# Signs, squares and their sums of a graph layer's closing algebra on ScalarE, block by block, and one wide product folded into a small one

## The chip, the cores and the metric

The kernel runs on one core of a Trainium2 chip. The metric is the device time of one execution in microseconds (us). The median of three runs of the kernel before is 815.14 us, with 815.1 and 816.52 as lowest and highest.

## What is computed

The reference is a chain of four graph layers on 4096 nodes with 64 features and a dense 4096 x 4096 matrix of zeros and ones. Each layer adds to `x` the result of a graph operator on the normalised, rectified `x`. The change touches only the last operator, a hyperbolic one:

```python
def weighted_midpoint_lincomb(A, X):
    gamma = lambda_x(X)
    num = A @ (gamma * X)
    den = A @ (gamma - 1.0)
    sgn = jnp.where(den >= 0.0, 1.0, -1.0)
    den = sgn * jnp.maximum(jnp.abs(den), DEN_EPS)
    two_mean = num / den
    mid = mobius_scalar_mul(0.5, two_mean)
    alpha = jnp.sum(A, axis=1, keepdims=True)
    return mobius_scalar_mul(alpha, mid)
...
XW = mobius_matvec(W, X)
AXW = weighted_midpoint_lincomb(A_hat, XW)
return expmap0(jax.nn.relu(logmap0(AXW)))
```

All the norms, tanh and artanh act on one length per node. What is needed for each node is the length of the sum vector, the length of its rectified part once the sign of the denominator is applied, the denominator and the row sum `alpha`; the result is a positive factor per node times the rectified vector.

## The kernel before

The 4096 nodes lie on 128 partitions in 32 blocks, each with 64 features along the free dimension. Layer 3 treats them in eight tiles of four blocks (CB = 4), numbered u = 0 to 7. For each tile, `sum3` multiplies the adjacency matrix by a 196-column matrix on TensorE: three bf16 parts of the 64 scaled features and of the denominator's column, 65 columns each, and a column of ones for `alpha`. The function `take3` then copies the first part out of PSUM on ScalarE and adds the other two on VectorE, and so makes a tile `n65` (128 x 4 x 65) and `alpha` (128 x 4).

`layer3` (lines 1678 to 1708) fixes the order on TensorE: the first half of the sums of tiles 0 to 2, then tiles 3 to 5 in full, then the second half of tiles 0 to 2, and last tiles 6 and 7. `summed` (line 1712) gathers finished tiles. Tiles 3, 4 and 5 form the first group that is closed together, tiles 0, 1 and 2 the second; tiles 6 and 7 are closed each alone. So `post3` (line 1740) runs four times, with nb = 12, 12, 4 and 4 columns of statistics.

Inside `post3`, the work of one tile is three wide operations and a reduction: `n65` times the sign of the denominator in place (line 1753), its square on ScalarE (1755), the square of its positive part on VectorE (1756), and one `tensor_reduce` over both (1759). Then follow small operations on all columns together: `lengths` takes a reciprocal root by VectorE steps, `artanh2` uses Ln on ScalarE and a polynomial on VectorE, and a tanh closes the factor `a`. While Ln and a table load run, `between` multiplies the rectified tile by its reciprocal length (1771). After the tanh, the tile is multiplied by `a` (1779), added to `x` (1781) and written out (1782).

The order of the instructions on each engine is settled when the program is built, by a planner, `Weave`. A generator such as `post3` yields its operations one by one; the planner books each with a planned cost (`Engine.cost`: on ScalarE 0.2 us and 0.9 ns per element, 0.08 more for an accumulator) and puts it between the operations of other pieces of work where its inputs should be ready. `take3` is called directly; it first lets ready pieces run and then enters its own operations. On the chip each engine works its list in that order: an operation that waits holds back all that stand behind it. Operations that go through the planner all have line 781 in the profile, so they are told apart by their tiles: `n` is `n65`, `ss` the sums of squares, `rc` the reciprocals and what artanh2 makes of them, `ny` the reciprocal lengths, `void` a dummy that loads a table ahead.

Of the kernel before, what the change touches and what calls it, by code (L numbers as in the profile page):

```python
# [12 lines left out]
AF = mybir.ActivationFunctionType  # L13
ALU = mybir.AluOpType
AX = mybir.AxisListType
# [556 lines left out]
CB = 4  # L572
# [219 lines left out]
def fast_kernel(ctx: ExitStack, tc: tile.TileContext, t: dict, out: bass.AP, flag: bass.AP):  # L792
# [36 lines left out]
    def b2(name, shape=(P, QB, D), dtype=F32):  # L829
        return b2p.tile(list(shape), dtype, tag="b2", name=name)  # L830

    def stat(name, n):
        return small.tile([P, ST], F32, tag="st", name=name)[:, :n]
# [3 lines left out]
    DV, AC, GP, SY = (Engine(weave, x.e, x.real, True) for x in (V, S_, G_, Y_))  # L837
# [79 lines left out]
    def rows(s, width=D):  # L917
        return s[:, :, None].to_broadcast([P, s.shape[1], width])
# [12 lines left out]
    def recip(v):  # L931
        r = stat("rc", v.shape[1])
        yield DV.reciprocal(r, v)
        return r
# [632 lines left out]
    def lengths(s):  # L1567

        yield DV.tensor_scalar(s, s, NORM_EPS2, None, op0=ALU.max)
        r = yield from rsqrt(s)  # L1570
        n = stat("norm", s.shape[1])
        yield DV.tensor_tensor(n, s, r, ALU.mult)
        return n, r
# [5 lines left out]
    def preload(func):  # L1579

        yield AC.activation(void, tab, func)

    def artanh2(x, between=()):

        nb = x.shape[1]
        xc = stat("axc", nb)
        yield DV.tensor_scalar(xc, x, ARTANH_BOUND, None, op0=ALU.min)
        r = stat("at", nb)
        yield DV.tensor_scalar(r, xc, -1.0, 1.0, op0=ALU.mult, op1=ALU.add)
        q = yield from recip(r)  # L1590
        yield DV.scalar_tensor_tensor(q, xc, 1.0, q, op0=ALU.add, op1=ALU.mult)
        yield AC.activation(q, q, AF.Ln)
        yield from preload(AF.Tanh)
        low = small.tile([P, ST], I32, tag="st", name="flow")[:, :nb]
        yield DV.tensor_scalar(low, xc, 0.25, None, op0=ALU.is_lt)
        x2, p = stat("x2", nb), stat("po", nb)
        yield DV.tensor_tensor(x2, xc, xc, ALU.mult)
        yield DV.tensor_scalar(p, x2, *(2.0 * c for c in ARTANH_POLY[:2]), op0=ALU.mult, op1=ALU.add)
        yield DV.tensor_tensor(p, p, x2, ALU.mult)
        for c in ARTANH_POLY[2:-1]:  # L1600
            yield DV.scalar_tensor_tensor(p, p, 2.0 * c, x2, op0=ALU.add, op1=ALU.mult)
        yield DV.scalar_tensor_tensor(p, p, 2.0 * ARTANH_POLY[-1], xc, op0=ALU.add, op1=ALU.mult)
        yield from between
        yield DV.copy_predicated(q, low, p)
        return q
# [106 lines left out]
    def summed(u, parts3, alone=False):  # L1712
        group.append((u, parts3))
        if alone or len(group) == 3:
            weave.add(post3(group[:]))
            group.clear()
# [23 lines left out]
    def post3(parts3):  # L1740

        nb = CB * len(parts3)
        sgn, den, ss = stat("sgn", nb), stat("den", nb), stat("ss", 2 * nb)
        part = [slice(i * CB, (i + 1) * CB) for i in range(len(parts3))]
        vs = [n65[:, :, :D] for u, (n65, al) in parts3]
        for h, v, (u, (n65, al)) in zip(part, vs, parts3):  # L1750
            d = n65[:, :, D]
            yield DV.tensor_scalar(sgn[:, h], d, 0.0, 2.0, op0=ALU.is_ge, op1=ALU.mult)
            yield DV.scalar_tensor_tensor(v, rows(sgn[:, h]), -1.0, v, op0=ALU.add, op1=ALU.mult)
            sq = b2("sq")
            yield AC.activation(sq[:, :CB, :], v, AF.Square)
            yield DV.scalar_tensor_tensor(sq[:, CB:, :], v, 0.0, v, op0=ALU.max, op1=ALU.mult)
            yield DV.tensor_scalar(den[:, h], d, -1.0, DEN_EPS, op0=ALU.mult, op1=ALU.max)
            yield DV.tensor_tensor(den[:, h], den[:, h], d, ALU.max)
            yield DV.tensor_reduce(ss.rearrange("p (k b) -> p k b", k=2)[:, :, h],
                                   sq.rearrange("p (k b) d -> p k b d", k=2), AX.X, ALU.add)  # L1760
        yield from preload(AF.Ln)
        rd = yield from recip(den)
        n, r = yield from lengths(ss)
        t = stat("t", nb)
        yield DV.tensor_tensor(t, n[:, :nb], rd, ALU.mult)
        ratio = stat("ratio", nb)

        def between():
            yield DV.tensor_tensor(ratio, n[:, nb:], r[:, :nb], ALU.mult)
            for h, v in zip(part, vs):  # L1770
                yield DV.scalar_tensor_tensor(v, v, 0.0, rows(r[:, nb:][:, h]), op0=ALU.max, op1=ALU.mult)

        a = yield from artanh2(t, between())
        for h, (u, (n65, al)) in zip(part, parts3):
            yield DV.scalar_tensor_tensor(a[:, h], a[:, h], 0.25, al, op0=ALU.mult, op1=ALU.mult)
        yield DV.scalar_tensor_tensor(a, a, ARTANH_MAX, ratio, op0=ALU.min, op1=ALU.mult)
        yield AC.activation(a, a, AF.Tanh)
        for h, v, (u, (n65, al)) in zip(part, vs, parts3):
            yield DV.tensor_tensor(v, v, rows(a[:, h]), ALU.mult)
            x = X[u // 2][:, (u % 2) * CB:(u % 2 + 1) * CB, :]  # L1780
            yield DV.tensor_tensor(x, x, v, ALU.add)
            yield SY.dma_start(out_nm[:, u * CB:(u + 1) * CB, :], x)
# [103 lines left out]
```

## Time and profile before

| | value |
|---|---|
| median of three runs | 815.14 us |
| span of the profiled execution | 813.9 us |
| TensorE busy | 776.2 us |
| VectorE busy | 638.4 us |
| ScalarE busy | 397.4 us |
| mean granted TensorE clock | 0.989 |

In the profile PE is TensorE, PEld its weight load, DVE VectorE, ACT ScalarE, SP the queue of the output's transfers. A row of a group or of the timeline names the engine, the operation, the tile that is written and the tiles that are read, their shapes and how many there are. A bracket shows for how long the engine was idle before it and what released it. The chain follows the last instruction back to what released each step.

### The profile page before, as it was taken

The numbers are of one execution on the slowest core, as the hardware profiler recorded it, in microseconds if no ns is written. First come the engines' busy times: TensorE is split into PE (matmuls) and PEld (weight loads), VectorE is DVE, ScalarE is ACT, GpSimd is POOL, SyncE is SP. The second block draws the span as 40 slices with busy tenths as digits, with TensorE's granted clock in tenths as the row PEclk, the third lists the DMA queues.
The fourth block names the chain that finished last, engine by engine and source line by source line (L and its number), as shares of the span: only waits on it lengthen the run. The fifth ranks groups of instructions, "written<-read, shape, count | busy, mean of one in ns | idle before, by whom it ended". The sixth has DMA issues, their size and how long they took to land.

```text
span 813.9 us, 12101 instructions
## 1 busy us (share of the span) xinstructions
PE 776.2 (95%) x4473; PEld 358.6 (44%) x4494; DVE 638.4 (78%) x1433; ACT 397.4 (49%) x613; POOL 61.1 (8%) x125
## 2 busy tenths in 40 slices
PE   5999999999999999999999999999999999999990
PEld 1334444444433333333333334444444444699990
DVE  6886777677678798888888888878779787774896
ACT  5655555565565657666666663022120254452333
POOL 3333232230000000000000000000000000000000
PEclk9999999999999999999999999999999999999995
DMA  9999999998301032022022016797879900000010
GB/s 220 151 176 168 201 160 192 196 161 186 104 14 39 0 118 65 0 91 65 0 66 91 0 33 239 287 319 229 283 263 356 273 23 4 2 2 1 2 41 17
DMA packets 43954, 98.39 MB, mean 121 GB/s; under 512 B 5104, under 2 KB 20464, under 8 KB 43888
## 3 DMA queue, kind: packets, MB, share of 16 engines
q1 hardware_dynamic: 25888, 78.98, 29.0%
q0 software_dynamic: 15840, 14.42, 18.9%
q10 hardware_dynamic: 2160, 4.14, 1.4%
q8 instruction: 37, 0.61, 0.3%
q14 instruction: 29, 0.24, 0.1%
HBM read 135.54 MB, written 5.24 MB: 173 GB/s over the span
## 4 chain that ended last, share of the span: by engine, by line
PE 90%; DVE 6%; ACT 1%; issue 1%; DMA 1%; SPq 0%; DVEq 0%; ACTq 0%
PE acc L976 54%; PE cnt L976 14%; PE score L976 14%; PE rz L976 2%; DVE sig L781 2%; PE ih L976 1%; PE ps_t L980 1%; PE ps_l L976 1%; DMA whole<-in_adjT 1%; PE ps_kq L976 1%; DVE ss L781 1%; DVE nt L781 1%; ACT sig L781 1%; PE ps_n L980 1%; DVE rc L781 0%
## 5 line engine op out<-in xcount | busy, mean ns | idle before, releaser
L781 ACT ACTIVATE sig<-score,fatt_add,fatt_mul 128x1024 f32<-128x1024 f32 x128 | 147.9, 1200 | 85.4 <-PE score L976 84.8
L781 DVE TENSOR_TENSOR sig<-sig,A 128x1024 f32<-128x1024 f32 x128 | 151.3, 1221 | 38.7 <-ACT sig L781 37.9
L781 DVE SCALAR_TENSOR_TENSOR whole<-whole 128x1024 f32<-128x1024 f32 x128 | 153.2, 1218 | 6.0 <-DMA whole<-in_adjT 5.6
L781 ACT ACTIVATE w<-cnt 128x512 int16<-128x512 f32 x198 | 111.2, 595 | 89.9 <-PE cnt L976 88.7
L976 PE MATMUL score<-qd,kT 64*128 64x512 f32 x512 | 128.2, 617 | 0.0
L976 PE MATMUL acc<-sig,S 128*64 128x512 f32 x512 | 125.4, 606 | 1.5 <-DVE sig L781 1.4
L976 PE MATMUL acc<-A,hm 128*128 128x512 fp8e4 x512 | 115.6, 379 | 0.8 <-DVE X L781 0.8
L976 PEld LDWEIGHTS <-hm 128*128 128x128 bf16 x768 | 73.5, 98 | 90.7 <-issue 10.5
L976 PE MATMUL cnt<-A,ftri 128*128 128x512 fp8e4 x256 | 97.9, 385 | 8.3 <-ACT A L781 8.3
L976 PE MATMUL cnt<-A,fupd 128*128 128x512 fp8e4 x248 | 95.6, 386 | 2.7 <-DVE w L781 1.6
L976 PE MATMUL acc<-S,A 128*128 128x196 bf16 x1024 | 88.2, 246 | 0.0
L976 PEld LDWEIGHTS <-A 128*128 128x128 fp8e4 x1024 | 87.1, 96 | 1.1 <-issue 0.8
L976 PEld LDWEIGHTS score<-qd,kT 64*128 64x128 f32 x512 | 43.7, 186 | 80.9 <-ACT sig L781 39.1
L781 DVE TENSOR_SCALAR w<-cnt 128x512 int16<-128x512 f32 x58 | 40.1, 691 | 45.5 <-PE cnt L976 41.1
L976 PE MATMUL acc<-w,hm 128*128 128x512 bf16 x235 | 71.0, 379 | 0.9 <-issue 0.2
L860 POOL DMA_DIRECT2D A<-in_adjT x110 | 59.3, 541 | 119.7 <-DMA A<-in_adjT 118.8
L976 PEld LDWEIGHTS acc<-sig,S 128*64 128x64 f32 x512 | 30.4, 136 | 82.7 <-issue 39.5
L976 PEld LDWEIGHTS <-lo 128*64 128x64 bf16 x768 | 36.9, 109 | 58.4 <-issue 36.4
L976 PE MATMUL acc<-A,lo 128*64 128x512 fp8e4 x512 | 59.3, 380 | 0.0
L781 ACT ACTIVATE mt<-acc 64x512 f32<-64x512 f32 x32 | 18.9, 591 | 66.2 <-PE acc L976 39.6
L976 PEld LDWEIGHTS <-fupd 128*128 128x128 bf16 x248 | 24.4, 98 | 46.0 <-issue 24.3
L1647 POOL MEMSET S<- 128x4 bf16 x8 | 0.9, 116 | 550.6 <-PE ps_l L976 505.4
(185 smaller groups left out, 649.5 us busy)
## 6 DMA issues: line engine op xcount, KB each, us to landing
whole<-in_adjT SPq DMA_DIRECT2D x128, 512.0 KB, 7.0
A<-in_adjT POOLq DMA_DIRECT2D x110, 128.0 KB, 13.2
qd<-qs SPq DMA_DIRECT2D x16, 128.0 KB, 3.0
mx<-gs SPq DMA_DIRECT2D x16, 128.0 KB, 8.1
xT<-gs SPq DMA_DIRECT2D x8, 256.0 KB, 7.6
x<-in_x SPq DMA_DIRECT2D x6, 256.0 KB, 6.1
xs<-x SPq DMA_DIRECT2D x4, 256.0 KB, 4.8
qs<-qT ACTq DMA_DIRECT2D x4, 256.0 KB, 6.3
```

The lines of the kernel that those rows point to most:

```text
L781: return fn(*args, **kw)
L860: nc.gpsimd.dma_start(A8[q][b // 2][:, b % 2, :], a)
L976: nc.tensor.matmul(o, lhsT, rhs, start=start, stop=stop, skip_group_check=True)
L980: nc.tensor.transpose(o, src, ident)
L1647: nc.gpsimd.memset(S3[q, c][:, :, 3 * e:], 1.0)
```

## The change

For the groups of three tiles (nb > CB) the wide operations of a tile on VectorE are replaced by three ScalarE activations for each of its four blocks of 64 features. The first squares the block and adds the squares up in the accumulator. The second applies the sign and rectifies in place, by the activation's per-partition scale. The third squares that and adds up. The sign itself becomes two small VectorE operations. The two tiles closed alone keep the old form of this part.

For all tiles, the wide product with the reciprocal length under Ln goes. That length is multiplied into the small factor `a` after the tanh instead, and the final wide product rectifies on the way. The aim is to take work from VectorE while TensorE is still at work on later tiles.

```diff
-        for h, v, (u, (n65, al)) in zip(part, vs, parts3):
+        for i, (h, v, (u, (n65, al))) in enumerate(zip(part, vs, parts3)):
             d = n65[:, :, D]
             yield DV.tensor_scalar(sgn[:, h], d, 0.0, 2.0, op0=ALU.is_ge, op1=ALU.mult)
-            yield DV.scalar_tensor_tensor(v, rows(sgn[:, h]), -1.0, v, op0=ALU.add, op1=ALU.mult)
             sq = b2("sq")
-            yield AC.activation(sq[:, :CB, :], v, AF.Square)
-            yield DV.scalar_tensor_tensor(sq[:, CB:, :], v, 0.0, v, op0=ALU.max, op1=ALU.mult)
+            if nb > CB:
+
+                yield DV.tensor_scalar(sgn[:, h], sgn[:, h], -1.0, None, op0=ALU.add)
+                for j in range(CB):
+                    k = i * CB + j
+                    yield AC.activation(sq[:, j, :], v[:, j, :], AF.Square, accum_out=ss[:, k:k + 1])
+                    yield AC.activation(v[:, j, :], v[:, j, :], AF.Relu, scale=sgn[:, k:k + 1])
+                    yield AC.activation(sq[:, j, :], v[:, j, :], AF.Square, accum_out=ss[:, nb + k:nb + k + 1])
+            else:
+                yield DV.scalar_tensor_tensor(v, rows(sgn[:, h]), -1.0, v, op0=ALU.add, op1=ALU.mult)
+                yield AC.activation(sq[:, :CB, :], v, AF.Square)
+                yield DV.scalar_tensor_tensor(sq[:, CB:, :], v, 0.0, v, op0=ALU.max, op1=ALU.mult)
             yield DV.tensor_scalar(den[:, h], d, -1.0, DEN_EPS, op0=ALU.mult, op1=ALU.max)
             yield DV.tensor_tensor(den[:, h], den[:, h], d, ALU.max)
-            yield DV.tensor_reduce(ss.rearrange("p (k b) -> p k b", k=2)[:, :, h],
-                                   sq.rearrange("p (k b) d -> p k b d", k=2), AX.X, ALU.add)
+            if nb == CB:
+                yield DV.tensor_reduce(ss, sq, AX.X, ALU.add)
...
             yield DV.tensor_tensor(ratio, n[:, nb:], r[:, :nb], ALU.mult)
-            for h, v in zip(part, vs):
-                yield DV.scalar_tensor_tensor(v, v, 0.0, rows(r[:, nb:][:, h]), op0=ALU.max, op1=ALU.mult)
...
         yield AC.activation(a, a, AF.Tanh)
+        yield DV.tensor_tensor(a, a, r[:, nb:], ALU.mult)
         for h, v, (u, (n65, al)) in zip(part, vs, parts3):
-            yield DV.tensor_tensor(v, v, rows(a[:, h]), ALU.mult)
+            yield DV.scalar_tensor_tensor(v, v, 0.0, rows(a[:, h]), op0=ALU.max, op1=ALU.mult)
             x = X[u // 2][:, (u % 2) * CB:(u % 2 + 1) * CB, :]
             yield DV.tensor_tensor(x, x, v, ALU.add)
```

## The prediction

> **What bounds the kernel now.** I read the page's busy times and chain first, then the stretches of the last 100 us, then the chain in order of time, and last the timeline of VectorE and ScalarE there. From the page:
>
> ```profile
> PE 776.2 (95%) x4473; PEld 358.6 (44%) x4494; DVE 638.4 (78%) x1433; ACT 397.4 (49%) x613; POOL 61.1 (8%) x125
> ...
> PE 90%; DVE 6%; ACT 1%; issue 1%; DMA 1%; SPq 0%; DVEq 0%; ACTq 0%
> ```
>
> TensorE sets the time for 90% of the span. The edit is in the closing algebra of layer 3, so only that stretch counts. The busy time by stretches, columns PE, PEld, DVE, ACT, POOL:
>
> ```profile
> 740.00:760.00 20.00, 20.00 (x237) 19.80 (x236) 8.35 (x27) 3.39 (x14) 0.00 (x0) 1.00 0.01 2
> ...
> 780.00:790.00 10.00, 10.00 (x121) 10.00 (x119) 9.10 (x46) 4.92 (x14) 0.00 (x0) 1.00 0.01 2
> 790.00:800.00 10.00, 3.18 (x38) 2.95 (x35) 8.56 (x42) 3.83 (x8) 0.00 (x0) 0.77 0.13 43
> 800.00:814.00 14.00, 0.00 (x0) 0.00 (x0) 7.28 (x37) 3.59 (x7) 0.00 (x0) 0.50 0.07 22
> ```
>
> TensorE has no gap and full clock up to 793.2, so nothing that the edit frees can bring that point forward. What follows is a tail of 20.7 us. The chain in order of time:
>
> ```profile
> 758.74 34.46 PE acc L976 x404
> 793.22 0.28 ACT n L781
> ...
> 794.21 0.27 DVEq L1706
> 794.48 0.09 issue
> 794.56 0.18 DVE rc L781
> ...
> 800.90 0.42 DVE X L781
> ...
> 807.50 0.44 DVE n L781
> 807.96 0.42 DVE X L781
> ```
>
> The tail is the two tiles closed alone, one after the other: tile 6 from its reciprocal at 794.56 to its residual sum at 800.90, tile 7 to 807.96, then the output. Tile 6's sums were complete long before (ScalarE copied its last part out of PSUM at 782.7, and VectorE had added it up by 786); it is late because VectorE was busy with the second group of three (tiles 0 to 2). The timeline shows where that group stood:
>
> ```profile
> 773.67 0.21 ACT L781 ACTIVATE rc<-rc 128x12 f32<-128x12 f32 x1 [1.76 <-DVE rc L781]
> ...
> 781.85 0.16 DVE L781 TENSOR_SCALAR ss<-ss 128x24 f32<-128x24 f32 x1
> ...
> 788.97 0.21 ACT L781 ACTIVATE rc<-rc 128x12 f32<-128x12 f32 x1 [1.76 <-DVE rc L781]
> ```
>
> The tanh of the first group (tiles 3 to 5) ends at 773.9; the second group's sums of squares are ready at 781.85; its tanh ends at 789.2, 4 us before TensorE ends. That slack is what the edit can spend.
>
> **What the Trainium skill says.** "ScalarE: Activation LUTs", section "What ACT_TABLE_LOAD costs", prices an ACTIVATE at 186 ns + 0.833 ns per element, 93 ns more for each per-partition pointer operand, and lets neighbours overlap by about 93 ns. This trace agrees: 128x256 squares take 415 ns and 128x512 ones 624 ns; the tanh with a bias pointer takes 719 ns where the plain square takes 624; a square at 719.46 lasting 0.62 is followed at 719.98, an overlap of 0.10. Its 1283 ns table load is the trace's 1.28 us. "VectorE: DVE Perf Modes", section "The TRN2 errata", says that many small tiles pay a fixed latency each; the slope from 415 to 624 ns leaves some 206 ns fixed, so a 64-wide ACTIVATE is mostly overhead. "Trace Analysis", section "Optimizing Scalar/DVE Operations", says moving work to ScalarE may pay if VectorE is saturated. VectorE is near that here (9.10 of 10), but the path also runs through ScalarE.
>
> **The change part by part.** Per tile of a group, VectorE loses the wide sign product (0.42), the relu-square (0.42), the reduction (0.68) and the wide product by the reciprocal length (0.36 in steady flow), and gains small operations of 0.16 to 0.2. That is some 1.5 us per tile, or 4.5 us per group. Pricing what ScalarE gains:
>
> - A 64-wide square by the trace's slope: 415 - 192 x 0.816 = 258 ns, 0.26. The relu has a pointer scale: 0.26 + 0.095 = 0.355.
> - The relu overwrites the block that the first square reads, and the second square reads what the relu wrote; both wait for ScalarE's own completion, so overlap is lost (gap about 0.03). Only the next block's first square can follow at once (overlap 0.10).
> - The read-out of an accumulator on ScalarE is not in this trace. VectorE's is: 0.08 us (at 757.34). Lower bound 0 (free), upper 0.20, the length of ScalarE's shortest ACTIVATE (void, 203 ns). I take 0.10, a shortest ACTIVATE less its overlap.
> - One block: 0.26 + 0.10 + 0.03 + 0.355 + 0.03 + 0.26 + 0.10 - 0.10 = 1.035 us. Bounds 0.835 and 1.235. Before, a whole tile of four blocks cost ScalarE 0.42.
>
> Now the walk, by the order in which the changed program lists each engine's instructions.
>
> *First group.* Its signs start at 757.74 as before; the relus can begin at 758.1. Twelve blocks are 12.4 us, the first square runs ahead (-0.3), and the evictions of tiles 0 and 1 stand between the blocks (2 x 0.55, from 760.65 to 761.2 in the old timeline). ScalarE ends at 771.3. PSUM is released by these evictions, at latest about 771 for tile 1, whose banks tile 7 needs only at some 782 (11 us of products before the end), so TensorE is not held.
>
> *Closing of the first group.* Old second group: 781.85 to the end of the logarithm's input at 785.44 is 3.59, less 0.52 for tile 6's sums inside it, 3.07. The sums of tile 2 (two of 0.35, one of 0.43, a small one) now stand there: 1.25. Then logarithm 0.3, table load and void 1.5, which covers the polynomial (some 1.45), then five small operations and the tanh: 6.5 in all. Tanh ends at 777.8.
>
> *Second group.* Its first square is queued behind that tanh on ScalarE. 12.4 us of blocks, 0.5 for tile 6's evictions, 0.3 of waiting for the third tile's sign (VectorE forms it only after tile 6's sums): 791.0. Its sums of squares are thus ready 9.2 us later than the 781.85 of before. From there 5.85 to the end of the tanh (3.07, then tile 6's relu-square 0.35 and the rest as above): 796.9.
>
> *Behind it on VectorE.* In order: a small one and tile 7's first-half sums (0.6), the new 128x12 product (0.2), tile 0's product and residual (0.8), tile 7's last sums (0.65 with a small one), the flag read (0.35, as 794.21 to 794.56), tile 1's product and residual (0.8), tile 6's reduction (0.6), tile 2's product and residual (0.8), and only then tile 6's reciprocal: 801.6 against 794.56, +7.0.
>
> *The two lone tiles.* They keep the old form but lose 0.35 of wide product under the logarithm and gain 0.2 after the tanh. In tile 6 the copy starts about 0.25 earlier; in tile 7 the void's end at 806.97 holds the tanh anyway. Net about -0.1 each, -0.2.
>
> Sum: 7.0 - 0.2 = +6.8 us, 815.14 + 6.8 = 822.0. With the bounds of the block: at 0.835 ScalarE ends the groups at 768.9 and 786.5, and the reciprocal starts at 797.1, +2.4 net; at 1.235, 773.7, 795.8 and 806.4, +11.6 net.
>
> **The rivals.** *A floor only.* Suppose ScalarE is as quick as needed. Tile 7's last sums still cannot start before 793.6, and behind them now stand 2.2 us (two products with residuals and the reduction) that VectorE had done before: 793.59 + 0.6 + 0.35 + 2.2 = 796.75, +2.2, less 0.2: 817.1. For it: ScalarE is busy only 4.92 of 10 us in the old stretch. Against: two rounds of twelve blocks with self-waits. *A dearer read-out.* If it costs 0.28 net twice, a block takes 1.4 us, 24 x 0.36 = 8.8 more: 831; nothing here shows it, nothing excludes it. *Faster.* The 4.5 us saved per group let tile 6 close before TensorE ends; only tile 7's chain is left, and the tail loses the 6.4 us from 794.56 to 800.90: 808.7. For it: VectorE is the busy engine, and tile 6's data is there at 786. Against: the listing puts tile 6's reciprocal behind tile 7's last sums. *No change:* the queue shift is absorbed and only -0.2 stays, 814.9; no slack in the tail speaks for it.
>
> **How the numbers follow.** ScalarE becomes the pace, 822.0: 0.64. The floor, 817.1 to 817.5: 0.19. Dearer read-out, 828 and more: 0.09. Faster, 808.7: 0.04. No change: 0.04. Predicted is the first. The range from 816.8 (the floor less some rounding) to 827.0 (a block at the upper bound) leaves out the last three, 0.17. A time within 0.2% lies between 813.5 and 816.8; the floor is barely over it, so I give 0.05 to same, 0.04 to faster, 0.91 to slower.
>
> **What would show it.** TensorE still ends at about 793. ScalarE is near full from 758 to 771 and from 778 to 791, with about 1.03 us per block; a read-out row of its own tells its price. VectorE waits for ScalarE at the maximum of the 24 sums, twice. Tile 6's reciprocal starts near 801.6, and the two lone chains take 6.8 and 7 us as before. I am wrong if a block takes under 0.85 us (then 817), if TensorE is held for a PSUM bank (then later still), or if tile 6's chain is under way before 794.

## The result

The changed kernel takes 821.9 us (821.06 to 822.9) against 815.26 us for the kernel before. The ratio is 1.0079, with a 95% interval from 1.0061 to 1.0097: slower by 0.8%, some 6.4 us. The prediction was 822.0 us. The executions of each kernel fall into two clusters more than 1 us apart (815.1 to 815.4 and 816.5 before; 821.1 and 822.7 to 822.9 changed), and the profiled ones took 815.69 and 821.12 us.

The spans of the two profiles differ by 5.3 us (819.2 and 813.9). In the profiles of the kernels below, the copy of tile 5 out of PSUM, which lies ahead of the changed code, starts up to 2.0 us earlier or later than in the kernel before; so wherever times of different kernels stand in one table below, they are shifted to have that copy at 754.91, where it is in the kernel before (at 754.82 in the changed one).

### The profile page after: what moved, and what is told of

The parts are those of the page before. It is cut to its first block, busy times and chain, and to the rows that moved or that the text cites. A ratio compares the mean times of both kernels' runs of the same rounds, so it can differ in the third digit from the quotient of the medians.

```text
span 819.2 us, 12202 instructions
## 1 busy us (share of the span) xinstructions
PE 776.2 (95%) x4473; PEld 358.6 (44%) x4494; DVE 630.1 (77%) x1417; ACT 416.5 (51%) x727; POOL 61.5 (8%) x125
## 4 chain that ended last, share of the span: by engine, by line
PE 84%; DVE 9%; ACT 4%; issue 2%; DMA 1%; SPq 0%; DVEq 0%; ACTq 0%
PE acc L976 49%; PE score L976 14%; PE cnt L976 14%; PE rz L976 2%; ACT sq L781 2%; DVE sig L781 2%; PE ih L976 1%; PE ps_t L980 1%; PE ps_l L976 1%; ACT n L781 1%; DMA whole<-in_adjT 1%; DVE nt L781 1%; DVE ss L781 1%; DVE n L781 1%; PE ps_kq L976 1%
```

## The profile after

The page of the changed kernel, busy times and shares of the chain by engine:

```profile
PE 776.2 (95%) x4473; PEld 358.6 (44%) x4494; DVE 630.1 (77%) x1417; ACT 416.5 (51%) x727; POOL 61.5 (8%) x125
...
PE 84%; DVE 9%; ACT 4%; issue 2%; DMA 1%; SPq 0%; DVEq 0%; ACTq 0%
```

TensorE does the same work in the same busy time. VectorE lost 8.3 us of work and ScalarE gained 19.1, and yet the chain's share of TensorE fell from 90% to 84%: the chain now leaves TensorE at 754.8, some 38 us before TensorE's end, and runs on over ScalarE and VectorE. The stretches show where, with the columns PE, PEld, DVE, ACT and POOL, for the changed kernel:

```profile
758.00:771.00 13.00, 13.00 (x156) 12.80 (x154) 5.34 (x28) 12.20 (x67) 0.00 (x0) 1.00 0.00 1
771.00:778.00 7.00, 7.00 (x85) 7.00 (x84) 6.02 (x35) 3.96 (x13) 0.00 (x0) 1.00 0.01 2
778.00:793.00 15.00, 15.00 (x178) 14.85 (x175) 7.53 (x37) 12.59 (x64) 0.00 (x0) 1.00 0.08 28
793.00:801.00 8.00, 0.09 (x1) 0.00 (x0) 7.08 (x34) 3.85 (x10) 0.00 (x0) 0.66 0.11 37
801.00:820.00 19.00, 0.00 (x0) 0.00 (x0) 11.13 (x62) 5.58 (x11) 0.00 (x0) 0.50 0.07 23
```

Two of these rows for the kernel before:

```profile
758.00:771.00 13.00, 13.00 (x155) 12.80 (x153) 12.04 (x56) 5.40 (x16) 0.00 (x0) 1.00 0.01 1
...
778.00:793.00 15.00, 15.00 (x179) 14.95 (x176) 13.86 (x63) 5.33 (x15) 0.00 (x0) 1.00 0.08 28
```

In both groups the load changed sides: VectorE from 12.0 to 5.3 and from 13.9 to 7.5 us, ScalarE from 5.4 to 12.2 and from 5.3 to 12.6. TensorE is not held anywhere before its end. One block on ScalarE, in the timeline of the changed kernel:

```profile
759.11 0.35 ACT L781 ACTIVATE n<-n,sgn 128x64 f32<-128x64 f32 x1
...
759.49 0.26 ACT L781 ACTIVATE sq<-n 128x64 f32<-128x64 f32 x1
759.65 0.19 ACT L781 ACTIVATION_READ_ACCUMULATOR sq<-n 128x1 f32 x1
759.74 0.24 ACT L781 ACTIVATE sq<-n 128x64 f32<-128x64 f32 x1
759.89 0.18 ACT L781 ACTIVATION_READ_ACCUMULATOR sq<-n 128x1 f32 x1
760.11 0.35 ACT L781 ACTIVATE n<-n,sgn 128x64 f32<-128x64 f32 x1
```

From one rectification to the next it is 1.00 us. Each accumulator output is an instruction of its own, called the read-out here. It begins 0.15 to 0.16 after its square and the next square 0.09 after it. Where the next instruction waits (759.74 to 760.11), square and read-out cost 0.37.

The four points that the prediction walked through, in the timeline of the changed kernel:

```profile
776.96 0.21 ACT L781 ACTIVATE rc<-rc 128x12 f32<-128x12 f32 x1 [0.35 <-DVE rc L781]
...
789.92 0.18 DVE L781 TENSOR_SCALAR ss<-ss 128x24 f32<-128x24 f32 x1 [2.79 <-ACT sq L781]
...
795.52 0.21 ACT L781 ACTIVATE rc<-rc 128x12 f32<-128x12 f32 x1 [0.39 <-DVE rc L781]
...
800.22 0.17 DVE L781 RECIPROCAL rc<-den 128x4 f32<-128x4 f32 x1
```

The bracket of the second line is the new wait: VectorE stands idle for 2.79 us until ScalarE has the second group's last sum. All that stands behind it waits too: the square of tile 6's positive part, whose input was ready at 786.6, runs at 793.06. At the first group's maximum of the sums (770.47) there is no such bracket, because VectorE had waited before: for the copies of tiles 0 and 1, which stand between the blocks on ScalarE (2.71, 1.22, 1.74 and 0.84 us). The reciprocal in the last line, which opens tile 6's closing, stood at 794.56 before. The end of the chain, in order of time:

```profile
798.03 0.44 DVE n L781
798.49 0.42 DVE X L781
798.91 0.60 DVE ss L781
799.51 0.34 DVE n L781
799.88 0.42 DVE X L781
...
813.12 0.43 DVE n L781
813.58 0.42 DVE X L781
```

The first five lines are work between tile 7's last sums and tile 6's reciprocal that VectorE had behind it in the kernel before.

## The experiments

All keep the code of the kernel before or of the changed one but for the lines shown. First the table that they are read from: when the second group's sums of squares are ready, tile 6's reciprocal, the last residual sum (all in us, aligned as said), and the measured ratio with its interval.

| kernel | sums ready | reciprocal | last residual | ratio |
|---|---|---|---|---|
| before | 781.85 | 794.56 | 807.96 | 1 |
| changed | 790.01 | 800.31 | 813.67 | 1.0079 (1.0061 to 1.0097) |
| fold alone | 781.28 | 791.96 | 806.72 | 0.9988 (0.9982 to 0.9995) |
| blocks alone | 789.88 | 800.22 | 814.40 | 1.0089 (1.0074 to 1.0104) |
| no read-outs | 787.54 | 797.84 | 811.20 | 1.0050 (1.0037 to 1.0064) |
| wide squares | 782.88 | 793.43 | 808.10 | 0.9999 (0.9992 to 1.0005) |
| by kind | 785.56 | 796.75 | 810.13 | 1.0024 (1.0015 to 1.0034) |
| first group only | 786.18 | 796.18 | 810.33 | 1.0032 (1.0021 to 1.0043) |
| second group only | 786.36 | 797.39 | 810.81 | 1.0039 (1.0026 to 1.0052) |
| fold, one chain for the last two | 781.29 | 796.45 (both tiles) | 803.31 | 0.9953 (0.9940 to 0.9965) |

TensorE's last product, aligned in the same way, ends between 793.17 and 793.19 in all ten: none of these edits moves it, and what they change is the tail behind it.

**The fold alone.** The kernel before with

```diff
-            for h, v in zip(part, vs):
-                yield DV.scalar_tensor_tensor(v, v, 0.0, rows(r[:, nb:][:, h]), op0=ALU.max, op1=ALU.mult)
...
         yield AC.activation(a, a, AF.Tanh)
+        yield DV.tensor_tensor(a, a, r[:, nb:], ALU.mult)
         for h, v, (u, (n65, al)) in zip(part, vs, parts3):
-            yield DV.tensor_tensor(v, v, rows(a[:, h]), ALU.mult)
+            yield DV.scalar_tensor_tensor(v, v, 0.0, rows(a[:, h]), op0=ALU.max, op1=ALU.mult)
```

> The kernel before with only the second part of the change: the wide product under the logarithm goes, its factor joins the small one after the tanh. Theory (the block-by-block sums on ScalarE cause the whole loss, the fold is harmless or helps): no small op of 0.2 us costs what a removed wide one gives, VectorE gains about 0.9 us per group, and this order lets tile 6's reciprocal stand before tile 7's last sums, near 792.5 us instead of 794.56; 814.3 us, between 813.6 and 815.0. Rival (the product after the tanh lengthens the path and costs in each of the four closings): above 815.6.

It gained: 0.12%, about 1.0 us, as the theory said. The timeline of VectorE in this kernel (its times are not shifted; TensorE ends 1.4 us later than in the kernel before):

```profile
793.35 0.17 DVE L781 RECIPROCAL rc<-den 128x4 f32<-128x4 f32 x1
...
795.16 0.61 DVE L781 TENSOR_TENSOR n<-n,acc 128x130 f32<-128x130 f32 x2
...
796.78 0.62 DVE L781 TENSOR_TENSOR n<-n,acc 128x130 f32<-128x130 f32 x2
```

Tile 6's reciprocal stands before both pairs of tile 7's sums: it runs ahead of TensorE's end, as the rival "faster" of the prediction wanted of the whole change. The gain from it is 1.2 us of the tail and not 6.4: tile 6's chain now starts 2.6 us earlier but has tile 7's sums in its middle and takes 7.39 us to its residual instead of 6.34, and tile 7's residual follows 0.3 us later behind it than before.

**The blocks alone.** The changed kernel with the lines of the fold undone.

> The changed kernel with the fold undone: blocks on ScalarE for the groups, the old wide product under the logarithm for all tiles. Theory: the same ScalarE pace of about 1.00 us per block, and the wide products of the groups back before each group's tanh, about 1 us each, less 0.2: tile 6's reciprocal near 802, 823.5 us. Rival (the fold carries part of the loss): below 821.

The ratio of 1.0089 is 7.3 us over the kernel before, 0.0010 above the changed kernel. The theory holds in the main: the blocks make the whole loss. The fold takes about 0.8 us of it back by the ratios, whose intervals overlap, and 0.7 by the last residual, much as it gains 1.0 alone. The expected 823.5 is 8.2 over, near the upper end of the interval (6.0 to 8.5 us), and the reciprocal came at 800.2, not near 802. The first group's tanh is later, as it should be with a wide product in front of it again (778.84 against 777.05, aligned), yet the second group's sums are ready as early as in the changed kernel and tile 6's reciprocal too. ScalarE's timeline in this kernel (not shifted) shows why: the second group's first square stands ahead of the first group's tanh here, and the tanh among the blocks.

```profile
777.74 0.24 ACT L781 ACTIVATE sq<-n 128x64 f32<-128x64 f32 x1
...
779.98 0.20 ACT L781 ACTIVATE rc<-rc 128x12 f32<-128x12 f32 x1
```

The extra time shows only behind the reciprocal: the maximum of tile 6's sums comes at 801.07 against 800.40, since a wide product and a residual stand between the reciprocal and it here, and the last residual at 814.40 against 813.67.

**No read-outs.**

```diff
                     yield AC.activation(sq[:, j, :], v[:, j, :], AF.Square, accum_out=ss[:, k:k + 1])
```

in both places became a square without an accumulator, but for the last of each group.

> The changed kernel, same order of instructions on every engine, with 46 of its 48 accumulator outputs left out (the sums of squares are then not formed, a constant stands in their place); only the last of each group is kept, for the wait. Theory (the pace of ScalarE sets the delay, with a floor given by the queue behind tile 7's last sums): a block falls from 1.00 to about 0.81 us, the second group's sums are ready some 4.5 us earlier, tile 6's reciprocal comes near 796.9 where the floor stops it, 818.4 us. Rival A (no floor): 817.3 or less. Rival B (the order alone makes the loss, whatever ScalarE's pace): within 0.5 us of 821.9.

The timeline of ScalarE shows blocks of 0.81 us, as expected:

```profile
758.75 0.35 ACT L783 ACTIVATE n<-n,sgn 128x64 f32<-128x64 f32 x1
759.13 0.40 ACT L783 ACTIVATE sq<-n 128x64 f32<-128x64 f32 x2
759.56 0.35 ACT L783 ACTIVATE n<-n,sgn 128x64 f32<-128x64 f32 x1
```

Rival B falls: with the order unchanged the loss went from 0.79% to 0.50%, which is 4.1 us where 3.1 were expected. The second group's sums came 2.5 us earlier and not 4.5. Waits that the changed kernel does not have, or has shorter, took back part of what the blocks saved:

```profile
771.19 0.39 ACT L783 ACTIVATE n<-acc 128x260 f32<-128x260 f32 x1 [1.38 <-PE acc L978]
...
782.07 0.28 ACT L783 ACTIVATE n<-acc 128x130 f32<-128x130 f32 x1 [0.49 <-PE acc L978]
...
784.01 0.35 ACT L783 ACTIVATE n<-n,sgn 128x64 f32<-128x64 f32 x1 [0.93 <-DVE sgn L783]
```

ScalarE waits for tile 2's product between the two groups, for tile 6's product among the blocks, and then for a sign that stands behind tile 6's sums on VectorE (0.93 us, against 0.45 in the changed kernel). The floor was therefore not reached, and this run does not decide on it.

**By kind.** The changed kernel with the loop over the blocks split in three; the second squares go to the other half of `sq`:

```diff
+                cols = [(j, i * CB + j) for j in range(CB)]
+                for j, k in cols:
+                    yield AC.activation(sq[:, j, :], v[:, j, :], AF.Square, accum_out=ss[:, k:k + 1])
+                for j, k in cols:
+                    yield AC.activation(v[:, j, :], v[:, j, :], AF.Relu, scale=sgn[:, k:k + 1])
+                for j, k in cols:
+                    yield AC.activation(sq[:, CB + j, :], v[:, j, :], AF.Square, accum_out=ss[:, nb + k:nb + k + 1])
```

> The changed kernel with the twelve activations of a tile in another order: four first squares, then four rectifications, then four second squares, so that no instruction waits for its neighbour. Same instructions, same read-outs, and VectorE's order the same but for two neighbouring swaps. Theory (of a block's 1.00 us about a quarter is ScalarE waiting for itself): a block falls to about 0.73 us, the second group's sums come some 4 us earlier, tile 6's reciprocal near the floor of 796.7, and the loss against before falls from 6.6 to 2.0 to 3.0 us. Rival (the price is in the instructions, not in their waits): the loss stays at 6 us or more.

The loss fell to 0.24%, 2.0 us, with the same 36 activations and 24 read-outs per group. ScalarE no longer waits for itself, in this kernel's timeline:

```profile
757.84 1.06 ACT L781 ACTIVATE n<-n,sgn 128x64 f32<-128x64 f32 x4 [1.90 <-DVE sgn L781]
758.81 0.24 ACT L781 ACTIVATE sq<-n 128x64 f32<-128x64 f32 x1
758.96 0.19 ACT L781 ACTIVATION_READ_ACCUMULATOR sq<-n 128x1 f32 x1
759.05 0.24 ACT L781 ACTIVATE sq<-n 128x64 f32<-128x64 f32 x1
```

Four rectifications take 1.06 us together instead of 0.35 each, and a square with its read-out 0.24: 0.24 + 0.24 + 0.24 = 0.72 per block, against 1.00. And here the floor shows. VectorE in the same kernel:

```profile
793.23 0.61 DVE L781 TENSOR_TENSOR n<-n,acc 128x130 f32<-128x130 f32 x2 [0.79 <-ACT alpha L781]
...
796.39 0.17 DVE L781 RECIPROCAL rc<-den 128x4 f32<-128x4 f32 x1
```

For 0.79 us VectorE waits for tile 7's last half to leave PSUM, and then 3.16 us of queue stand before tile 6's reciprocal, at 796.75 when aligned: to a hundredth the 796.75 of the prediction's floor. A quicker ScalarE could not help this order any more. So of the changed kernel's loss some 4.4 us go with ScalarE's pace, and some 2.0 with the work that the order puts behind tile 7's last sums.

**Wide squares.**

```diff
+                yield AC.activation(sq[:, :CB, :], v, AF.Square)
+                for j in range(CB):
+                    k = i * CB + j
+                    yield AC.activation(v[:, j, :], v[:, j, :], AF.Relu, scale=sgn[:, k:k + 1])
+                yield AC.activation(sq[:, CB:, :], v, AF.Square)
```

in place of the three activations per block, with the reduction on VectorE again.

> The changed kernel with the same work on ScalarE in fewer instructions: per tile one wide square, four rectifying activations with the sign as scale, one wide square; the reduction is back on VectorE. Theory (ScalarE's loss is the number of instructions and their waits for one another, not the elements): a tile costs ScalarE 1.9 instead of 4.0 us, the first group's sums are ready near 765 as before, and the time is that of the fold alone or a little less, 814.0 us (813.2 to 815.0). Rival (moving the sign and both squares to ScalarE is what costs): above 817.

A tile costs ScalarE about 1.9 us, and the loss against the kernel before is gone, so the rival, above 817, falls. The expected gain of 1.2 us did not come: 0.9999, between 0.9992 and 1.0005. This kernel has the fold too, so against the fold alone it still costs some 0.9 us by the ratios and 1.4 by the last residual. The timeline of the second group says why:

```profile
779.23 0.69 DVE L781 TENSOR_REDUCE ss<-sq 128x8 f32<-128x512 f32 x1 [1.37 <-ACT sq L781]
...
780.29 1.06 ACT L781 ACTIVATE n<-n,sgn 128x64 f32<-128x64 f32 x4 [0.79 <-DVE den L781]
...
781.84 0.69 DVE L781 TENSOR_REDUCE ss<-sq 128x8 f32<-128x512 f32 x1 [1.37 <-ACT sq L781]
```

The two engines take turns: VectorE's reduction of one tile stands before the sign of the next, so ScalarE waits 0.79 us for the sign (the bracket names `den`, which follows the sign on VectorE) and VectorE 1.37 us for the squares: 2.61 us per tile, where it was 1.87 in the kernel before. The expectation counted ScalarE's work and not this exchange.

**One group at a time.** The changed kernel with the blocks only where `parts3[0][0] == 3`, or only where it is 0:

```diff
+        blocks_on_act = parts3[0][0] == 3
...
-            if nb > CB:
+            if blocks_on_act:
```

> Blocks on ScalarE for the first group of three only, the old wide form for the second; the fold for all. Theory (delays of the two groups add up along one chain, each some 3 to 4 us): the first group's tanh ends near 777 as in the changed kernel, the second group takes VectorE's old time, less the wide products; tile 6's reciprocal about 2 us later than before: +2.0 us against before, between +1.0 and +3.0. Rival (only the group next to the tail costs, the first one's delay is absorbed before TensorE ends): between -1.2 and +0.5 us.

> Blocks on ScalarE for the second group only; the fold for all. Theory: the first group closes as early as with the fold alone, the second group's twelve blocks on ScalarE take 12 us from about 774 and end near 787; here tile 6's wide operations stand behind tile 7's last sums as well, so its reciprocal comes near 798: +3.5 us against before, between +2.0 and +4.5. Rival (the whole loss comes from this group): +5.5 us or more.

Measured 0.32% (2.6 us) and 0.39% (3.2 us), both inside what the theory gave and outside both rivals. Against the fold alone these are 0.0044 and 0.0051, and their sum of 0.0095 is about the 0.0091 of the changed kernel: the delays of the two groups nearly add up (by the last residual 3.6 and 4.1 us, together 7.0). Here a group far ahead of TensorE's end is no safer a place than the next one. In the changed kernel the next one's first square stands right behind its tanh on ScalarE (777.07 behind 776.96); the kernel with the blocks alone has another order there, so this is the planner's choice.

**The fold, and one chain for the last two tiles.** The kernel before with the fold, and `post3` divided: a part `wide3` makes the sign, the squares and the sums of one tile, and it is started for tile 6 as soon as that tile is summed; for tile 7 it runs after TensorE's end, and then the rest of `post3` closes both on eight columns.

```diff
+            if u == 6:
+                last.extend(stat(n, 2 * CB * k) for n, k in (("sgn", 1), ("den", 1), ("ss", 2)))
+                weave.add(wide3(group[:], *last, 0))
+            else:
+                weave.add(post3(group[:], last))
+                group.clear()
```

> The kernel before with the fold, and the two lone tiles closed by one chain of small operations: tile 6's wide operations are done as soon as its sums are there, then tile 7's, then both go through the closing together on eight columns. The blocks on ScalarE are left out. Theory (after TensorE's end the time is two serial chains of small operations on VectorE, 6.3 and 5.9 us, and their length hardly depends on the number of columns): one chain less, minus tile 7's wide operations that now stand alone: about -5 us against before, between -3.5 and -6. Rival (the lone chains overlap with work that must be done anyway): above -1.5 us.

It is the fastest here: 0.9953, some 3.8 us below the kernel before, within the expected band if short of its middle. The tail in its timeline:

```profile
796.09 0.19 DVE L781 RECIPROCAL rc<-den 128x8 f32<-128x8 f32 x1
...
802.95 0.42 DVE L781 TENSOR_TENSOR X<-X,n 128x256 f32<-128x256 f32 x1
```

From the reciprocal to the last residual it is 6.86 us for two tiles. In the kernel before, each had its own such stretch, 6.34 us (794.56 to 800.90) and 5.85 us (802.11 to 807.96). The small operations last 0.14 to 0.20 us on 4, 8 or 16 columns alike, so inside the chain a second tile costs only its wide product and residual. Tile 7's own wide operations now stand in front of the chain, which starts at 796.45 aligned, where tile 6's alone started at 794.56 in the kernel before.

## Why the prediction was right

The number was right, 822.0 against 821.9, and so was the mechanism: ScalarE became the pace, and the blocks alone carry the loss. Step by step:

- *One block*: 1.035 predicted, 1.00 measured. The square is 0.25 (said 0.26), the rectification 0.35 (0.355), and the read-out, the unknown between 0 and 0.20, adds about 0.09 (0.10) although its row shows 0.19. The value taken, a shortest ACTIVATE less its overlap, was right; at its full row the read-out would have put the block near the upper bound, about 1.2, still short of the rival "dearer".
- *First group*: ScalarE's blocks end at 770.4 (said 771.3), the tanh at 777.2 (777.8). The evictions between the blocks did not hold TensorE.
- *Second group*: sums ready at 789.9 (791.0), tanh ends at 795.7 (796.9). Of the 1.1 us at the sums, 24 blocks at 0.035 make 0.84, and the evictions between them 0.7 (said 1.1 and 0.5, were 0.6 and 0.3). The first group's closing, 6.7 and not 6.5, and the wait for the third tile's sign, 0.4 and not 0.3, took some of it back.
- *The queue behind it*: tile 6's reciprocal at 800.2 (801.6), later by 5.7 us and not by 7.0. The stretch from the second group's sums to its tanh was put at 5.85 and measured 5.81, although the parts that the walk names for it add up to 5.6.
- *The lone tiles*: said to gain 0.2 us, gained 0.04: from tile 6's reciprocal to the last residual it is 13.36 against 13.40 us. In tile 6 the predicated copy came 0.24 earlier relative to the reciprocal, as said, and the new small product gave it back.

One of the prediction's signs did not come: VectorE waits for ScalarE at the maximum of the 24 sums once and not twice.

By these steps the sum is 5.6 us, by the spans 5.3, by the comparison of all executions 6.4. So the exact match of the total has luck in it: the walk was about 1.2 us too long, and the measured difference is about 0.8 us more than the steps show. The two profiled executions are themselves 5.4 us apart, and the interval of the comparison, four executions of each kernel, reaches from 5.0 to 7.9 us; it holds both figures, so the 0.8 us need no cause of their own, and none is shown.

Of the rivals, the floor was real, though not what bounds the changed kernel: the order by kind sits on it at 796.75, 2.0 us slower than before. "Dearer read-out" falls by the block without read-outs, 0.81 against 1.00 us. "Faster" falls for the whole change, and its reason is half true: the fold alone does bring tile 6 forward, and gains 1.0 us. "No change" falls by the interval.

## What to carry to other kernels

Before moving wide work to an idle-looking engine, price it per instruction and per wait on itself: 36 activations of 64 columns in dependent triples took 1.00 us per block, 4.0 per tile, where the same activations ordered by kind took 0.72 per block, and where the one square over a tile's four blocks in the kernel before took ScalarE 0.42 per tile, with the rest on VectorE. An engine that is half idle on average can still be the path if the moved work stands in a chain that others queue behind, and a floor can be read from the queue alone: here 3.2 us of work had slipped behind the last thing that waits for TensorE. Where the tail is a chain of small operations whose time does not depend on their width, joining two such chains can gain more than thinning either: here 3.8 us for both, of which the thinner chain alone gave 1.0.

## What had not been expected

- An accumulator output on ScalarE shows as a row of 188 ns on average, more than twice VectorE's 0.08 us, and yet it costs only 0.09 us beside the next square, and taking both out of a block saves 0.19 us, no more.
- Rectifications with a pointer scale last 0.35 us, but four in a row take 1.06: 0.24 for each after the first. So some 0.11 of the 0.35 us is time that only a successor that waits for the result pays; in the dependent order it begins 0.03 us after the row's end.
